# Row sums of the attention weights: part of them moved from ScalarE to GpSimd and VectorE, with pinned orders

## The chip, the cores and the metric

One NeuronCore of a Trainium2 chip runs the whole kernel. TensorE multiplies matrices, VectorE and GpSimd work element by element, ScalarE evaluates functions, SyncE (SP) issues most DMAs. Each engine takes its instructions in order from a queue of its own; semaphores tie the queues together. The metric is the time of one execution in device microseconds; the shown number is the median of several runs.

## The reference

The network has four layers on four images of 128 channels and 64 x 64 pixels: a state-space layer with convolutions, a 3 x 3 convolution, an attention block with expert feed-forward, and a linear attention with expert feed-forward. The change lies in the attention of the third layer alone. An image has 4096 tokens, 16 heads and a width of 8 per head. Query, key and value are the same tensor:

```python
qkv = _qz_ring(heads + rx_theta)
q = jnp.transpose(qkv, (0, 2, 1, 3))
scores = jnp.einsum('bhsd,bhtd->bhst', q, q) / np.sqrt(D)
attn = jax.nn.softmax(scores, axis=-1)
ctx = jnp.einsum('bhst,bhtd->bhsd', attn, q)
```

Since query and key are the same, the matrix of scores is symmetric. Its exponentials are needed once for each pair of tokens, used for both the row and the column, and the softmax needs their sums over both directions.

## The kernel before

`attention` (line 909) runs once per image, between stages (`prepare`, `feed_forward`) that compute the heads and what follows. The 4096 tokens are cut into four blocks of queries, j = 0 to 3, of 1024 tokens, and sixteen blocks of keys, m, of 256 tokens. Only blocks with m >= 4j are computed. A block with m // 4 > j lies off the diagonal ("behind" in the code) and serves both directions; the four with m // 4 = j serve one. `pairs(j)` gives the order of the m: behind a few of the first kind comes one of the diagonal. A head has 16 + 12 + 8 + 4 = 40 steps, of which 24 are "behind"; an image has 16 heads and 640 steps.

One step (loop at line 1073) consists of:

- four matmuls `score` for the 2 x 1024 scores of a pair of key halves, into two PSUM tiles of three;
- two exponentials on ScalarE (line 1094), `ex`, 128 x 1024 each. In "behind" steps each also accumulates the sum of its row into `dacc` (`accum_out`); the chip then runs a second, short instruction that reads the accumulator out;
- in "behind" steps two 32 x 32-block transposes on VectorE (line 1098) into `turned`. A `turned` tile takes the eight transposes of four blocks m, and there are two such tiles;
- `turns` (line 1015): once all eight transposes of a group are made and a step has passed, TensorE multiplies them with values that GpSimd has spread (`turned_v`), one to three `turn`s of four matmuls in a step, eight turns for a group, summed in `acc_ps`. Behind a group's last turn VectorE copies or adds `acc_ps` to `acc` (lines 1006, 1008);
- `weigh` (line 1026) of the step before: the exponentials times values, summed in `ctx_ps` over all m of a j. At the last m of a j the turned sums are added by `place` matmuls, VectorE copies `ctx_ps` to `ctx` (line 1057), and SP stores it with eight DMAs.

`load` (line 921) fetches keys and queries of the next head by 32 DMAs into `raw`, and GpSimd casts them to the matmul type (line 940). `load_values` (line 944) fetches values by four DMAs and spreads them on GpSimd (line 954), three times a head. At the end of an image one reduce over `dacc` (line 1110) gives the sums.

TensorE's order in this stage is the order of the program (`manual_schedule`, line 1207). The orders of the other engines come from the framework's scheduler, which sorts by its own estimates. On VectorE that has put, at the first step of a new j, the two transposes of this step in front of the copy of the `ctx_ps` that was just finished.

Of the kernel before, what the change touches and what calls it, by code (L numbers as in the profile page):

```python
# [9 lines left out]
F32 = mybir.dt.float32  # L10
F32R = mybir.dt.float32r
I32 = mybir.dt.int32
AF = mybir.ActivationFunctionType
ALU = mybir.AluOpType
AX = mybir.AxisListType
PSUM = bass.MemoryType.PSUM

P = 128
NB = 4
HW = 64  # L20
L = HW * HW
CH = 512
# [752 lines left out]
def layer2_attention(K, xd, dpool, w):  # L775

    nc, tc, mm = K.nc, K.tc, K.mm
# [4 lines left out]
    with ExitStack() as ctx:  # L782
# [126 lines left out]
        def attention(qt, dsum, big, work, pssc, psctx, psacc):  # L909
# [11 lines left out]
            def load(h, queues=(nc.sync, nc.sync)):  # L921

                out = []
                for keys in (True, False):
                    t = work.tile([P, L // 2], F32R, name="keys" if keys else "queries")
                    raw = work.tile([P, L // 2], F32, name="raw")
                    n = P if keys else CH
                    for p in range(2):  # L930
                        for c in range(2):
                            for k in range(4):
                                r = unit(p, c).start + HD * k
                                src = head_d[k // 2 if keys else k % 2, HD * h : HD * h + HD]
                                at = p if keys else c
                                queues[not keys].dma_start(
                                    out=raw[r : r + HD].rearrange("d (m s) -> d m s", s=n),
                                    in_=src.rearrange("d (m z s) -> d m z s", z=2, s=n)[:, :, at],
                                )
                    nc.gpsimd.tensor_copy(t, raw)  # L940
                    out.append(t)
                return out

            def load_values(h, j):


                v = work.tile([P, 4 * BT, HD], F32, name="v")
                for a in range(4):
                    nc.sync.dma_start(
                        out=v[32 * a : 32 * a + 32],  # L950
                        in_=value_d[h, :, j].rearrange("s q t d -> s (q t) d"),
                    )
                t = work.tile([P, 4 * BT, 4, HD], F32, name="turned_v")
                nc.gpsimd.tensor_tensor(  # L954
                    t,
                    v.unsqueeze(2).to_broadcast([P, 4 * BT, 4, HD]),
                    quarter.unsqueeze(1).to_broadcast([P, 4 * BT, 4, HD]),
                    ALU.mult,
                )
                return t  # L960
# [8 lines left out]

            steps = [(h, j, m) for h in range(NH) for j in range(NJ) for m in pairs(j)]  # L970
            heads = {0: load(0, (nc.sync, nc.scalar))}
            values = {(0, 0): load_values(0, 0)}
            order = [(h, j) for h in range(NH) for j in range(NJ - 1)]
            cps = psctx.tile([P, CH], F32, name="ctx_ps")
            aps = psacc.tile([P, 2, BT, 32], F32, name="acc_ps")
# [4 lines left out]
            def turn():  # L980

                r, h, j, i, td, _, sums = groups[0]
                if r == 0:
                    sums = groups[0][-1] = aps[:, halves[0] % 2]
                    halves[0] += 1
                groups[0][0] += 1
                tv = values[h, j]
                for g in range(4):
                    n = 4 * r + g
                    q, t = divmod(n, BT)  # L990
                    at = 32 * (4 * t + q)
                    mm(
                        sums[32 * g : 32 * g + 32],
                        tv[:, n].rearrange("p a d -> p (a d)"),
                        td[:, :, at : at + 32],
                        start=r == 0,
                        stop=r == BT - 1,
                    )
                if r < BT - 1:
                    return False  # L1000
                groups.pop(0)
                if i == 1:
                    accs[h] = work.tile([P, NJ - 1, BT, 32], F32, name="acc")
                at = accs[h][:, i - 1]
                if j == 0:
                    nc.vector.tensor_copy(at, sums)  # L1006
                else:
                    nc.vector.tensor_tensor(at, at, sums, ALU.add)
                if i == NJ - 1:
                    after = order.index((h, j)) + 2  # L1010
                    if after < len(order):
                        values[order[after]] = load_values(*order[after])
                return True

            def turns(n, ready):
# [10 lines left out]
            def weigh(h, j, m, exs):  # L1026

                last = m == 4 * j + 3
                first = m == (4 * j + 4 if j < NJ - 1 else 4 * j)
                for p in range(2):  # L1030
                    at = (h * NTT + 2 * m + p) * (HD + 1)
                    for c in range(2):
                        mm(
                            cps[unit(p, c), :],
                            qt[:, at : at + 32],
                            exs[p][:, c, :],
                            start=first,
                            stop=last and j == 0,
                        )
                if not last:  # L1040
                    return
                if j > 0:
                    while any(g[1] == h and g[3] == j for g in groups):
                        turn()
                    for k in range(2):
                        for p in range(2):
                            for c in range(2):
                                a = 2 * p + k
                                mm(
                                    cps[unit(p, c), :].rearrange("r (t a s) -> r t a s", a=4, s=32)[:, :, a],  # L1050
                                    place[:, a, :],
                                    accs[h][:, j - 1, 4 * c : 4 * c + 4],
                                    start=False,
                                    stop=k == 1,
                                )
                u = work.tile([P, CH], F32, name="ctx")
                nc.vector.tensor_copy(u, cps)  # L1057
                for p in range(2):
                    for c in range(2):
                        cols = slice((2 * j + c) * CH, (2 * j + c + 1) * CH)  # L1060
                        r = unit(p, c).start
                        nc.sync.dma_start(out=num_d[p, HD * h : HD * h + HD, cols], in_=u[r : r + HD])
                        nc.sync.dma_start(out=den_d[p, h : h + 1, cols], in_=u[r + HD : r + HD + 1])

            values[order[1]] = load_values(*order[1])


            starts = [n for n, (h, j, m) in enumerate(steps) if m // 4 > j and m % 4 == 0]
# [1 line left out]
            begun = {}  # L1070
            turned = None
            past = None
            for n, (h, j, m) in enumerate(steps):
                keys, queries = heads[h]
                if n == 0 or h != steps[n - 1][0]:
                    if h + 1 < NH:
                        heads[h + 1] = load(h + 1)
                behind = m // 4 > j
                if n in ends:
                    turned = work.tile([P, BT, 2 * CH], F32, name="turned")  # L1080
# [2 lines left out]
                for p in range(2):  # L1083
                    for c in range(2):
# [2 lines left out]
                            keys[unit(p, c), m * P : (m + 1) * P],  # L1087
                            queries[unit(p, c), j * CH : (j + 1) * CH],
                        )
                exs = []  # L1090
                for p in range(2):
                    ex = work.tile([P, 2, CH], F32, name="ex", bufs=6)
                    t = 2 * m + p
                    nc.scalar.activation(  # L1094
                        ex, sps[p], AF.Exp, scale=scale, accum_out=dacc[:, j, h, t : t + 1] if behind else None
                    )
                    if behind:
                        nc.vector.transpose(turned[:, t % BT, :], ex.rearrange("p c s -> p (c s)"))  # L1098
                    exs.append(ex)
                turns(n, lambda g: begun[id(g[4])] < n - 1)  # L1100
                if past is not None:
                    weigh(*past)
                past = (h, j, m, exs)
                if behind and m % 4 == 3:
                    begun[id(turned)] = n
# [1 line left out]
            while groups:  # L1107
                turn()
            weigh(*past)
            nc.vector.tensor_reduce(dsum, dacc.rearrange("p j h t -> p t h j"), AX.X, ALU.add)  # L1110

        def feed_forward(b, dsum, work, psum):
# [75 lines left out]
        for b in range(NB + 1):  # L1188
            with tc.tile_pool(name="l2_big", bufs=1) as big:
# [12 lines left out]
                with (  # L1202
                    tc.tile_pool(name="l2_work", bufs=2) as work,
                    tc.tile_pool(name="l2_pssc", bufs=3, space=PSUM) as pssc,
                    tc.tile_pool(name="l2_psctx", bufs=1, space=PSUM) as psctx,
                    tc.tile_pool(name="l2_psacc", bufs=1, space=PSUM) as psacc,
                    tc.manual_schedule(engines={mybir.EngineType.PE}),
                ):
                    attention(qt, past, big, work, pssc, psctx, psacc)

# [432 lines left out]
```

## Time and profile before

| | |
|---|---|
| median of 3 runs | 11391.87 us (11381.06 to 11405.95) |
| the profiled execution | 11405.55 us, span 11403.8 us |
| the four attention stages | 1424, 1427, 1427, 1425 us |
| busy over the whole span | TensorE 81%, VectorE 64%, ScalarE 66%, GpSimd 23% |
| busy in the second attention stage | TensorE 94%, VectorE 68%, ScalarE 89%, GpSimd 12% |
| granted TensorE clock in it | 0.99 |

PE is TensorE (PEld its weight loads), DVE VectorE, ACT ScalarE, POOL GpSimd, SP SyncE. A row of the largest groups names line, engine, operation, output<-input, shapes and count; then the busy time in us and the mean of one in ns; then how long the engine stood idle ahead of such instructions, and for whom it waited. L89 is the helper for all matmuls, so matmuls are told apart by their tiles. In the view of waits the numbers are us in total, times, and the longest. In the timeline they are the start, the duration, engine, line, operation, tiles, and in brackets the idle time ahead of it.

### The profile page before, as it was taken

The numbers are of one execution on the slowest core, as the hardware profiler recorded it, in microseconds if no ns is written. First come the engines' busy times: TensorE is split into PE (matmuls) and PEld (weight loads), VectorE is DVE, ScalarE is ACT, GpSimd is POOL, SyncE is SP. The second block draws the span as 40 slices with busy tenths as digits, with TensorE's granted clock in tenths as the row PEclk, the third lists the DMA queues.
The fourth block names the chain that finished last, engine by engine and source line by source line (L and its number), as shares of the span: only waits on it lengthen the run. The fifth ranks groups of instructions, "written<-read, shape, count | busy, mean of one in ns | idle before, by whom it ended". The sixth has DMA issues, their size and how long they took to land. (4 is left out here: it accounts for less than half of the span.)

```text
span 11403.8 us, 182690 instructions
## 1 busy us (share of the span) xinstructions
PE 9270.3 (81%) x71376; PEld 3448.3 (30%) x71376; DVE 7274.7 (64%) x7758; ACT 7509.0 (66%) x11610; POOL 2630.9 (23%) x1711
## 2 busy tenths in 40 slices
PE   5777777777759999958999967999967999976766
PEld 2222223222123333323333322333322333323433
DVE  2687687687736666656666655666655666654464
ACT  2564554554428888848888847888846888852331
POOL 0466455565611111121111121111121111110000
PEclk8888878888679999979999979999979999988898
DMA  3322322322122121122211122122122112112103
GB/s 84 89 63 56 95 61 66 86 63 66 49 57 34 32 32 32 34 66 35 37 31 32 24 74 38 32 33 36 24 71 41 31 31 33 31 55 87 49 16 133
DMA packets 524322, 581.50 MB, mean 51 GB/s; under 512 B 106232, under 2 KB 329536, under 8 KB 520896
## 3 DMA queue, kind: packets, MB, share of 16 engines
q1 hardware_dynamic: 520896, 565.61, 21.6%
q8 instruction: 561, 9.19, 0.3%
q10 hardware_dynamic: 2560, 4.20, 0.3%
q14 instruction: 305, 2.50, 0.1%
HBM read 373.96 MB, written 76.55 MB: 40 GB/s over the span
## 5 line engine op out<-in xcount | busy, mean ns | idle before, releaser
L1094 ACT ACTIVATE ex<-score 128x1024 f32<-128x1024 f32 x5120 | 5015.9, 1040 | 665.4 <-PE score L89 657.3
L1098 DVE STREAM_TRANSPOSE turned<-ex 128x1024 f32<-128x1024 f32 x3072 | 3596.9, 1219 | 1595.6 <-ACT ex L1094 1453.1
L89 PE MATMUL ctx_ps<-ex,qt 128*32 128x512 f32 x20480 | 2872.8, 603 | 230.4 <-DVE ctx L1057 229.7
L89 PE MATMUL acc_ps<-turned,turned_v 128*32 128x256 f32 x24576 | 1750.8, 387 | 99.2 <-DVE acc L1006 49.7
L89 PE MATMUL score<-queries,keys 32*128 32x512 f32 x10240 | 1365.0, 500 | 185.4 <-POOL queries L940 182.1
L641 DVE TENSOR_TENSOR_SCAN hs<-decay,carry,hs 128x512 f32<-128x512 f32 x1024 | 1248.0, 1263 | 151.2 <-ACT decay L640 141.9
L640 ACT ACTIVATE decay<-dt,a_neg 128x512 f32<-128x512 f32 x1024 | 699.9, 690 | 883.0 <-DVE hs L641 879.4
L954 POOL TENSOR_TENSOR turned_v<-v,quarter 128x1024 f32<-128x1024 f32 x192 | 456.4, 2378 | 3549.9 <-PE acc_ps L89 3432.7
L89 PEld LDWEIGHTS score<-queries,keys 32*128 32x128 f32 x10240 | 529.3, 183 | 2262.3 <-issue 1589.0
L647 POOL TENSOR_TENSOR hs<-hs,c_sb 128x1024 f32<-128x1024 f32 x512 | 1201.4, 2367 | 49.1 <-DMA c_sb<-c_d 29.4
L89 PEld LDWEIGHTS ctx_ps<-ex,qt 128*32 128x32 f32 x20480 | 683.1, 110 | 832.8 <-DVE ctx L1057 310.3
L89 PEld LDWEIGHTS acc_ps<-turned,turned_v 128*32 128x32 f32 x24576 | 607.3, 108 | 780.2 <-issue 514.9
L89 PE MATMUL y_ps<-hs,pair 128*64 128x512 f32 x2048 | 658.8, 761 | 224.4 <-POOL hs L647 224.3
L637 DVE TENSOR_TENSOR hs<-dtx,b_ps 128x2048 f32<-128x2048 f32 x256 | 581.5, 2271 | 316.8 <-PE b_ps L89 227.8
L1094 ACT ACTIVATION_READ_ACCUMULATOR ex<-score 128x1 f32 x3072 | 680.4, 221 | 0.0
L89 PE MATMUL ln_var<-ln_sq,mean 128*128 128x512 f32 x448 | 296.3, 748 | 220.5 <-ACT ln_sq L104 185.1
L89 PE MATMUL b_ps<-dbc,spread 32*128 32x512 f32 x512 | 343.8, 756 | 149.6 <-DVE hs L637 149.6
L89 PE MATMUL conv<-under,deep 96*32 96x512 f32 x1536 | 283.2, 715 | 74.4 <-DMA under<-xp 54.6
L89 PEld LDWEIGHTS y_ps<-hs,pair 128*64 128x64 f32 x2048 | 138.3, 161 | 674.2 <-POOL hs L647 418.0
L940 POOL CAST keys<-raw 128x2048 fp32r<-128x2048 f32 x64 | 121.1, 1892 | 917.9 <-DMA raw<-head_d 865.2
L644 POOL COPY carry<-hs 128x4 f32<-128x4 f32 x256 | 64.9, 253 | 1108.9 <-DVE hs L641 1096.0
L1057 DVE COPY ctx<-ctx_ps 128x512 f32<-128x512 f32 x256 | 169.7, 663 | 198.5 <-PE ctx_ps L89 198.5
(340 smaller groups left out, 8583.1 us busy)
## 6 DMA issues: line engine op xcount, KB each, us to landing
raw<-head_d SPq DMA_DIRECT2D x1984, 64.0 KB
c_sb<-c_d SPq DMA_DIRECT2D x512, 128.0 KB
dt<-dt SPq DMA_DIRECT2D x128, 256.0 KB
dtx<-dtx SPq DMA_DIRECT2D x128, 256.0 KB
w<-in_L_ffn_weight SPq DMA_DIRECT2D x32, 1024.0 KB
w<-in_L_ffn_weight SPq DMA_DIRECT2D x128, 256.0 KB
under<-xp SPq DMA_DIRECT2D x384, 66.0 KB
under<-fp SPq DMA_DIRECT2D x384, 66.0 KB
```

The costliest lines, as they stand in the source:

```text
L89: self.nc.tensor.matmul(out, lhsT, rhs, start=start, stop=stop)
L637: nc.vector.tensor_tensor(hs, dtx2, bb.unsqueeze(1).to_broadcast([P, NQ, CH]), ALU.mult)
L640: nc.scalar.activation(ex, dt2[:, q, :], AF.Exp, scale=a_neg[:, q, g : g + 1])
L641: nc.vector.tensor_tensor_scan(hs[:, q, :], ex, hs[:, q, :], carry[:, g, q : q + 1], ALU.mult, ALU.add)
L644: nc.gpsimd.tensor_copy(carry[:, g, :].unsqueeze(2), hs[:, :, CH - 1 : CH])
L647: nc.gpsimd.tensor_tensor(at, at, cs.unsqueeze(1).to_broadcast([P, 2, CH]), ALU.mult)
L940: nc.gpsimd.tensor_copy(t, raw)
L954: nc.gpsimd.tensor_tensor(t, v.unsqueeze(2).to_broadcast([P, 4 * BT, 4, HD]), quarter.unsqueeze(1).to_broadcast([P, 4 * BT, 4, HD]), ALU.mult,
L1057: nc.vector.tensor_copy(u, cps)
L1094: nc.scalar.activation(ex, sps[p], AF.Exp, scale=scale, accum_out=dacc[:, j, h, t : t + 1] if behind else None)
L1098: nc.vector.transpose(turned[:, t % BT, :], ex.rearrange("p c s -> p (c s)"))
```

## The change

- 15 of the 24 "behind" steps of a head (`folded`: eight in j=0, four in j=1, three in j=2) no longer accumulate on ScalarE. `fold` has GpSimd add the two halves of each row of the exponentials, 2 x 1024 to 2 x 512, and again to 2 x 256 (`quarters`). Five steps later VectorE reduces these to two columns of `dacc`.
- The two exponentials of a step share one tile, `ex`, of four buffers; before there were six of half the size.
- VectorE and GpSimd now also run in the order of the program in this stage.
- `turns` and `weigh` stand ahead of the exponentials and transposes in the program. TensorE's order stays; on VectorE the copies of `acc_ps` and `ctx_ps` come ahead of that step's transposes.
- Keys and queries are loaded directly into their tiles and cast in place, at steps 28 and 32 of the head ahead (`rounded`); before, they went through `raw`. Values are spread three steps after their loads are issued (`waiting`), where before the scheduler placed it.

```diff
@@ load, load_values
-                    raw = work.tile([P, L // 2], F32, name="raw")
+                    raw = t.bitcast(F32)
...
-                    nc.gpsimd.tensor_copy(t, raw)
                     out.append(t)
                 return out
+
+            def rounded(t):
+
+                nc.gpsimd.tensor_copy(t, t.bitcast(F32))
...
+                return v
+
+            def spread_values(v):
                 t = work.tile([P, 4 * BT, 4, HD], F32, name="turned_v")
@@ turn
-                        values[order[after]] = load_values(*order[after])
+                        waiting.append((now[0] + 3, order[after], load_values(*order[after])))
@@ before the loop
+            folds = []
+
+            def folded(j, m):
+
+                return ((m - 4) % 3 < 2, m % 2 == 0, m % 4 < 3)[j]
+
+            def fold(n, exs, at):
+                hs = work.tile([P, 2, CH], F32, name="folded", bufs=1)
+                qs = work.tile([P, 2, CH // 2], F32, name="quarters", bufs=6)
+                nc.gpsimd.tensor_tensor(hs, exs[:, :, 0], exs[:, :, 1], ALU.add)
+                nc.gpsimd.tensor_tensor(qs, hs[:, :, 0 : CH // 2], hs[:, :, CH // 2 :], ALU.add)
+                folds.append((n + 5, qs, at))
@@ the loop over steps
-                if n == 0 or h != steps[n - 1][0]:
-                    if h + 1 < NH:
+                if h + 1 < NH:
+                    if n % per == 0:
                         heads[h + 1] = load(h + 1)
+                    if n % per in (per - 12, per - 8):
+                        rounded(heads[h + 1][n % per == per - 8])
+                while waiting and n >= waiting[0][0]:
+                    _, at, v = waiting.pop(0)
+                    values[at] = spread_values(v)
...
-                exs = []
+                turns(n, lambda g: begun[id(g[4])] < n - 1)
+                if past is not None:
+                    weigh(*past)
+                exs = work.tile([P, 2, 2, CH], F32, name="ex", bufs=4)
+                aside = behind and folded(j, m)
                 for p in range(2):
-                    ex = work.tile([P, 2, CH], F32, name="ex", bufs=6)
+                    ex = exs[:, p]
                     t = 2 * m + p
+                    summed = behind and not aside
                     nc.scalar.activation(
-                        ex, sps[p], AF.Exp, scale=scale, accum_out=dacc[:, j, h, t : t + 1] if behind else None
+                        ex, sps[p], AF.Exp, scale=scale, accum_out=dacc[:, j, h, t : t + 1] if summed else None
                     )
                     if behind:
                         nc.vector.transpose(turned[:, t % BT, :], ex.rearrange("p c s -> p (c s)"))
-                    exs.append(ex)
-                turns(n, lambda g: begun[id(g[4])] < n - 1)
-                if past is not None:
-                    weigh(*past)
+                if aside:
+                    fold(n, exs, dacc[:, j, h, 2 * m : 2 * m + 2])
+                while folds and folds[0][0] <= n:
+                    _, qs, at = folds.pop(0)
+                    nc.vector.tensor_reduce(at, qs, AX.X, ALU.add)
@@ the stage's pools
-                    tc.manual_schedule(engines={mybir.EngineType.PE}),
+                    tc.manual_schedule(
+                        engines={mybir.EngineType.PE, mybir.EngineType.DVE, mybir.EngineType.Pool}
+                    ),
```

More of the change, by code (lines that the diff above doesn't have):

```diff
@@ L971, in attention @@
             heads = {0: load(0, (nc.sync, nc.scalar))}
-            values = {(0, 0): load_values(0, 0)}
+            for t in heads[0]:
+                rounded(t)
+            values = {(0, 0): spread_values(load_values(0, 0))}
+            waiting = []
             order = [(h, j) for h in range(NH) for j in range(NJ - 1)]
@@ L1035, in weigh @@
                             qt[:, at : at + 32],
-                            exs[p][:, c, :],
+                            exs[:, p, c, :],
                             start=first,
@@ L1063, in weigh @@
                         nc.sync.dma_start(out=den_d[p, h : h + 1, cols], in_=u[r + HD : r + HD + 1])
-            values[order[1]] = load_values(*order[1])
+            values[order[1]] = spread_values(load_values(*order[1]))
+            folds = []
[7 more added lines that the diff above has]
+                folds.append((n + 5, qs, at))
             starts = [n for n, (h, j, m) in enumerate(steps) if m // 4 > j and m % 4 == 0]
@@ L1072, in attention @@
             past = None
+            now = [0]
+            per = len(steps) // NH
             for n, (h, j, m) in enumerate(steps):
+                now[0] = n
                 keys, queries = heads[h]
-                if n == 0 or h != steps[n - 1][0]:
-                    if h + 1 < NH:
+                if h + 1 < NH:
+                    if n % per == 0:
                         heads[h + 1] = load(h + 1)
+                    if n % per in (per - 12, per - 8):
[3 more added lines that the diff above has]
+                    values[at] = spread_values(v)
                 behind = m // 4 > j
@@ L1109, in attention @@
             weigh(*past)
+            for _, qs, at in folds:
+                nc.vector.tensor_reduce(at, qs, AX.X, ALU.add)
             nc.vector.tensor_reduce(dsum, dacc.rearrange("p j h t -> p t h j"), AX.X, ALU.add)
```

## The prediction

> **What bounds the kernel now.** I first read the slices and the largest groups of the profile page. The changed code is the attention stage, which runs four times, once per image. Asked for those four stretches, the trace gives 1424, 1427, 1427 and 1425 us, half of the span. The rest of the kernel isn't touched and I leave it at 11403.8 - 5703 = 5701 us.
>
> ```profile
> core 0: us, PE busy (x) PEld busy (x) DVE busy (x) ACT busy (x) POOL busy (x), PEclk, DMA share, GB/s
> 5148.00:6575.00 1427.00, 1343.70 (x14568) 480.52 (x14562) 967.97 (x928) 1269.86 (x2048) 170.17 (x78) 0.99 0.18 31
> ```
>
> Busy shares in it: TensorE 94%, ScalarE 89%, VectorE 68%, GpSimd 12%. Two engines are near full, so I looked at the groups.
>
> ```profile
> L1094 ACT ACTIVATE ex<-score 128x1024 f32<-128x1024 f32 x5120 | 5015.9, 1040 | 665.4 <-PE score L89 657.3
> L1098 DVE STREAM_TRANSPOSE turned<-ex 128x1024 f32<-128x1024 f32 x3072 | 3596.9, 1219 | 1595.6 <-ACT ex L1094 1453.1
> L89 PE MATMUL ctx_ps<-ex,qt 128*32 128x512 f32 x20480 | 2872.8, 603 | 230.4 <-DVE ctx L1057 229.7
> L89 PE MATMUL acc_ps<-turned,turned_v 128*32 128x256 f32 x24576 | 1750.8, 387 | 99.2 <-DVE acc L1006 49.7
> ...
> L647 POOL TENSOR_TENSOR hs<-hs,c_sb 128x1024 f32<-128x1024 f32 x512 | 1201.4, 2367 | 49.1 <-DMA c_sb<-c_d 29.4
> ...
> L1094 ACT ACTIVATION_READ_ACCUMULATOR ex<-score 128x1 f32 x3072 | 680.4, 221 | 0.0
> ```
>
> ScalarE waits 657.3 us for scores, TensorE 229.7 us for a copy on VectorE. The view of waits says how often:
>
> ```profile
> ACT ex L1094 <- PE score L89: 657.3, 983, 11.1
> ...
> PE ctx_ps L89 <- DVE ctx L1057: 229.7, 188, 2.1
> ```
>
> That is 1.22 us a time, three times a head (64 heads, 192 places). The timeline at one such place, the move from j=1 to j=2:
>
> ```profile
> 5566.33 2.37 DVE L1098 STREAM_TRANSPOSE turned<-ex 128x1024 f32<-128x1024 f32 x2 [0.92 <-ACT ex L1094]
> ...
> 5566.78 0.62 PE L89 MATMUL ctx_ps<-acc,place 128*32 128x128 f32 x16
> ...
> 5567.88 1.94 ACT L1094 ACTIVATE ex<-score 128x1024 f32<-128x1024 f32 x2 [0.58 <-PE score L89]
> 5568.62 0.65 DVE L1057 COPY ctx<-ctx_ps 128x512 f32<-128x512 f32 x1
> ...
> 5569.33 1.07 PE L89 MATMUL ctx_ps<-ex,qt 128*32 128x512 f32 x8 [0.93 <-DVE ctx L1057]
> ```
>
> The sums are ready at 5567.40; their copy stands behind two transposes until 5568.62, and TensorE stands still to 5569.33.
>
> Per step I took the distance between the first exponentials of neighbouring steps, from their starts in the trace, averaged over heads (steps counted 0 to 39). A head lasts 89.25 us. Steps with a transpose and one turn or none last 1.99 us (4, 5, 19, 20, 25, 26, 32, 34), diagonal ones 1.82: ScalarE's pace. Steps with two turns last 2.30 to 2.35: TensorE's pace. The move to a new j costs most: 3.77 (step 1), 3.30 (17), 3.05 (29); step 22 has 2.84. From the timeline TensorE needs 0.43 for scores, 0.95 for context, 0.445 a turn and 0.6 for the place products: 1.38, 1.83, 2.28 with no, one, two turns; 40 x 1.38 + 48 x 0.445 + 3 x 0.6 = 78.4 us a head at least.
>
> **What the Trainium skill says.** "ScalarE: Activation LUTs", What ACT_TABLE_LOAD costs: back-to-back ACTIVATEs overlap by about 93 ns. The trace agrees: 1.04 us each, 0.91 apart without accumulation, 1.00 with it. So a read of the accumulator, 221 ns in its row, costs only 0.09 us of ScalarE's pace. "GPSIMD Engine Reference", 1. Specifications: the SBUF interfaces are shared with VectorE, with contention for VectorE instructions in a 2-port mode or with two SBUF inputs. Transposes have one input, and 145 of them that lie wholly under GpSimd work took 1.21 us, against 1.22 for those clear of it. "VectorE: DVE Perf Modes", Rules for kernel authors: expect 1x of `tensor_reduce`. The trace has one of 512 elements:
>
> ```profile
> L413 DVE TENSOR_REDUCE sm<-sc x32: 651/659/686, 118.9 to 2226.2; 128x32 f32<-128x512 f32 x32
> ```
>
> **The change part by part**, in us a head, times 64.
>
> *Reads removed.* 15 of 24 steps lose two reads: 30 x 0.09 = 2.7 if ScalarE set the pace everywhere. It doesn't where a folded step has two turns (8, 9, 12, 13, 16, 22) or lies in a move (28). Left are 0, 1, 4, 5, 19, 25, 30 and 32: 8 x 0.18 = 1.4. Gain 1.4, between 0.5 and 2.7.
>
> *Copies ahead of transposes.* At steps 0, 16 and 28 the copy is now ahead of the two transposes. It starts when the sums are ready and takes 0.66; meanwhile TensorE has 0.43 of scores and mostly a turn, so about 0.15 of each 1.22 is left. Gain 3 x 1.07 = 3.2; bounds 2 and 3.6. What is late next: transposes of that step, which now wait for TensorE's sums.
>
> *Row sums on VectorE.* 15 reduces at about 0.62 (0.66 less the overlap of neighbours) are 9.3: VectorE goes from 968 to 968 + 240 x 0.62 = 1117 of about 1390 us per image, 80%. Idle time of 1.46 us between transposes covers them in j=2. In j=0, steps 0 to 15 hold 24 transposes 1.17 apart, six reduces and 1.4 of copies, 33.2 us, against 35.4 that these steps last now: no cover to spare. Behind a reduce wait the next transposes and the copy of the accumulators; for both TensorE waits at the first turn of the next group. Three places:
> - Step 16. Six transposes from step 12 on are 7.0, the copy of step 15 0.4, ending some 0.3 after TensorE wants them today. The reduces of steps 13 and 14 stand in front of that copy: 1.2 later.
> - Step 22. Today VectorE is late by 2.84 - 2.28 = 0.56. Now the transposes of step 16 wait for the copy that waits for two turns, and the reduces of 17 and 18 add 1.24; the diagonal step takes up part. Loss 0.7.
> - Step 6. The head's first transposes wait behind the copy, and ScalarE brings step 4 and 5 sooner. Loss 0.6.
>
> Together 2.5; bounds 0.5 (idle time takes most) and 5.5 (a reduce of this form near 1 us, as the `dsum` reduce with its 2.92 us for 1536 elements would give, and every one of them on the path).
>
> *Folds on GpSimd.* 2.37 (the L647 row) + 1.27 (a 128x512 sum on GpSimd, L1182) = 3.64; fifteen are 54.6. With three spreads at 2.38 and two casts at 1.89 that is 65.5 of 87 us. Cost nothing while the exponential four steps later still finds its buffer free. Tightest: step 5 needs the first half of step 1's fold; fold 0, the spread now placed at step 1 and that half are 8.4 after step 0, the exponential is due at 7.5. The 0.9 is hidden, since step 6 waits for transposes anyway. Without that cover: 0.9 a head, 58 us. Bounds 0 and 1.
>
> *Casts and loads.* The loads write keys and queries directly, casts come at steps 28 and 32, in front of those steps' folds. A head's 32 loads take 32 x 0.65 = 21 us of SP's queue, begun when the head before last has finished its scores; they have landed some 35 us before the cast. The queries' cast ends near step 33, needed seven steps later. On SP three value loads now stand in a row ahead of the context stores of j=2; the third waits for a spread at step 38, the stores are ready at 37, and their buffer is next wanted a head later. Nothing; if the loads were late, GpSimd would stop with all folds behind it.
>
> *Batch start.* Each image's first scores wait 45 us for loads and casts (182.1 us in all); these are the same transfers. Nothing.
>
> Sum: 1.4 + 3.2 - 2.5 = 2.1 a head, x 64 = 134 us. The profiled execution took 11405.55 (span 11403.8): 11271. It stood 13.7 above the median of the runs: **11257 us**.
>
> **Rivals.**
> 1. *VectorE has room.* Reduces fall into its idle time and the copies stay prompt. For it: 68% busy now, 1453 us waiting for ScalarE. Against: j=0 has no such room. 1.4 + 3.2 = 4.6, 294 us: 11098.
> 2. *VectorE, in its fixed order, sets the pace* (other side). Place: first turns at steps 6, 16, 22. It decides once the lateness there passes 4.6 a head instead of 2.5. For it: j=0 at 33.2 of 35.4, copies that wait for TensorE with transposes behind them. Against: the measured 0.66. At 5.5 it loses 0.9 x 64 = 58: 11450.
> 3. *GpSimd sets the pace*: needs (87 - 10.9) / 15 = 5.1 a fold where rows say 3.64. At 5.6, 10.9 + 84 = 94.9 a head, 5.7 over today's: 11392 + 365 = 11757.
> 4. *No change*: gain and lateness cancel, 11392.
>
> **How the numbers follow.** Forecast (gains of 30 to 230) 0.53; rival 1 (beyond) 0.24; rival 4 0.07; rival 2 0.13; rival 3 0.03. Within 0.2% (23 us, about what this measurement can tell from no change) 0.07, faster 0.77, slower 0.16. Range: down to 11080, which holds most of rival 1, up to 11430, part of rival 2; about 0.1 is left out on each side. The forecast's own range is 11165 to 11360.
>
> **What would show it.** Right: 1152 reads left; waits of context for its copy from 229.7 to below 60; reduces near 0.66; waits of `acc_ps` for VectorE above 99; steps 4 and 5 at 1.85, steps 1, 17 and 29 together some 3 us shorter, 16 and 22 longer. Wrong: ScalarE waiting for GpSimd at all; transposes above 1.25; step 16 no longer than today (rival 1).

## The result and the profile after

The changed kernel took 11269.95 us in the median of four runs (11248.79 to 11277.42), against 11396.6 in four runs of the kernel before. The ratio is 0.9887, with a 95% interval of 0.9869 to 0.9905: 1.1% faster, 127 us. The forecast was 11257. The profiled execution was the fastest of the four, with a span of 11247.0; the one profiled before was among the slower of its kernel, so the two spans differ by more, 157 us.

The stretches of the four attention stages are now 1391, 1392, 1391 and 1391 us. Their sum of 5565 is 138 under that of before; the other 19 us of the two spans lie outside the attention stages. The second stretch, with the same columns as before:

```profile
core 0: us, PE busy (x) PEld busy (x) DVE busy (x) ACT busy (x) POOL busy (x), PEclk, DMA share, GB/s
5108.00:6500.00 1392.00, 1327.58 (x14569) 482.03 (x14570) 1098.28 (x1167) 1232.73 (x1568) 1046.23 (x558) 1.00 0.19 32
```

VectorE went from 68% to 79% busy, GpSimd from 12% to 75%, and ScalarE stayed at 89% of a shorter stretch. The largest groups of the page after:

```profile
L1129 ACT ACTIVATE ex<-score 128x1024 f32<-128x1024 f32 x5120 | 4917.9, 1027 | 674.6 <-issue 282.4
L1133 DVE STREAM_TRANSPOSE turned<-ex 128x1024 f32<-128x1024 f32 x3072 | 3586.1, 1217 | 504.4 <-ACT ex L1129 375.5
...
L89 PE MATMUL ctx_ps<-ex,qt 128*32 128x512 f32 x20480 | 2817.8, 596 | 22.1 <-DVE ctx L1066 21.4
L89 PE MATMUL acc_ps<-turned,turned_v 128*32 128x256 f32 x24576 | 1750.7, 387 | 215.8 <-DVE acc L1015 161.9
...
L1138 DVE TENSOR_REDUCE dacc<-quarters 128x2 f32<-128x512 f32 x960 | 622.2, 653 | 0.0
```

The context matmuls wait 21.4 us for their copy instead of 229.7, and ahead of the `acc_ps` matmuls TensorE is idle for 215.8, nearly all of it for VectorE, instead of 99.2. Transposes kept their 1.22 us although GpSimd now works beside most of them. The reduces take 0.653.

The distance in us between the first exponentials of neighbouring steps, as in the prediction, shows where it went. It is averaged over the heads of each image but the first and the last. The steps that the text needs are shown, of both kernels and of six of the runs told of below; a head is the sum of all 40 steps.

| step | before | after | order alone | old order | spread behind | reduces at diagonals | held to 21 | sums left out |
|---|---|---|---|---|---|---|---|---|
| 1 | 3.77 | 1.87 | 2.02 | 3.66 | 1.86 | 1.86 | 1.86 | 1.86 |
| 4 | 1.99 | 2.67 | 1.99 | 1.81 | 1.81 | 2.67 | 1.81 | 1.81 |
| 5 | 1.99 | 1.82 | 1.99 | 1.81 | 1.81 | 1.83 | 1.81 | 1.81 |
| 6 | 2.09 | 2.08 | 2.12 | 2.43 | 2.48 | 2.08 | 2.48 | 2.49 |
| 11 | 1.99 | 2.04 | 1.99 | 2.59 | 2.04 | 2.04 | 2.04 | 1.99 |
| 16 | 2.47 | 3.62 | 2.47 | 3.62 | 3.62 | 2.52 | 2.51 | 2.46 |
| 17 | 3.30 | 2.25 | 2.35 | 2.25 | 2.25 | 2.24 | 2.25 | 2.36 |
| 22 | 2.84 | 3.53 | 2.84 | 3.50 | 3.52 | 3.53 | 2.91 | 2.88 |
| 28 | 2.75 | 2.83 | 2.74 | 3.41 | 2.82 | 2.82 | 2.82 | 2.79 |
| 29 | 3.05 | 1.83 | 1.94 | 2.21 | 1.83 | 1.83 | 1.83 | 1.94 |
| 36 | 3.48 | 3.48 | 3.48 | 4.07 | 3.48 | 3.48 | 3.48 | 3.42 |
| head | 89.25 | 86.90 | 85.32 | 90.42 | 86.43 | 85.80 | 84.71 | 84.77 |

The three moves to a new j (steps 1, 17, 29) are 4.2 us a head shorter. Steps 4, 16 and 22 are 2.5 longer, and the others together 0.7 shorter. That makes 2.35 a head; over all heads, the first and last ones too, it is 2.18, or 139 us for 64, as the stretches say. Step 16 in the timeline of the kernel after, VectorE's lines first, TensorE's behind them:

```profile
5488.61 0.64 DVE L1138 TENSOR_REDUCE dacc<-quarters 128x2 f32<-128x512 f32 x1
5489.18 2.36 DVE L1133 STREAM_TRANSPOSE turned<-ex 128x1024 f32<-128x1024 f32 x2
5491.46 0.64 DVE L1138 TENSOR_REDUCE dacc<-quarters 128x2 f32<-128x512 f32 x1
5492.02 0.41 DVE L1015 COPY acc<-acc_ps 128x256 f32<-128x256 f32 x1
...
5490.70 0.51 PE L89 MATMUL score<-queries,keys 32*128 32x512 f32 x4
5492.49 1.07 PE L89 MATMUL acc_ps<-turned,turned_v 128*32 128x256 f32 x16 [1.29 <-DVE acc L1015]
```

Two reduces stand in front of the copy, one of them directly, and TensorE idles 1.29 us for that copy. At step 22 it idles as long, 1.23 in the mean, for the next such copy. Step 4 is late by another engine. ScalarE's line comes first, then GpSimd's:

```profile
5468.12 2.86 ACT L1129 ACTIVATE ex<-score 128x1024 f32<-128x1024 f32 x3 [0.73 <-POOL folded L1084]
...
5459.66 2.38 POOL L1084 TENSOR_TENSOR folded<-ex 128x1024 f32<-128x1024 f32 x1 [10.02 <-ACT ex L1129]
5462.12 1.28 POOL L1085 TENSOR_TENSOR quarters<-folded 128x512 f32<-128x512 f32 x1
5463.37 2.38 POOL L960 TENSOR_TENSOR turned_v<-v,quarter 128x1024 f32<-128x1024 f32 x1
5465.70 2.39 POOL L1084 TENSOR_TENSOR folded<-ex 128x1024 f32<-128x1024 f32 x1
```

The exponential of step 5 reuses the tile of step 1. It starts when GpSimd's fold has read that tile, and that fold stood behind the fold of step 0 and the spread.

### The profile page after: what moved, and what is told of

It is laid out like the page before. It is cut to its first block, busy times and chain, and to the rows that moved or that the text cites. A ratio compares the mean times of both kernels' runs of the same rounds, so it can differ in the third digit from the quotient of the medians.

```text
span 11247.0 us, 183547 instructions
## 1 busy us (share of the span) xinstructions
PE 9199.9 (82%) x71376; PEld 3451.5 (31%) x71376; DVE 7810.3 (69%) x8718; ACT 7359.6 (65%) x9690; POOL 6136.6 (55%) x3631
## 3 DMA queue, kind: packets, MB, share of 16 engines
q14 instruction: 307, 2.51, 0.1%
## 5 line engine op out<-in xcount | busy, mean ns | idle before, releaser
L1129 ACT ACTIVATE ex<-score 128x1024 f32<-128x1024 f32 x5120 | 4917.9, 1027 | 674.6 <-issue 282.4
L1084 POOL TENSOR_TENSOR folded<-ex 128x1024 f32<-128x1024 f32 x960 | 2293.4, 2389 | 1260.2 <-ACT ex L1129 1226.9
L89 PE MATMUL ctx_ps<-ex,qt 128*32 128x512 f32 x20480 | 2817.8, 596 | 22.1 <-DVE ctx L1066 21.4
L89 PE MATMUL acc_ps<-turned,turned_v 128*32 128x256 f32 x24576 | 1750.7, 387 | 215.8 <-DVE acc L1015 161.9
L1085 POOL TENSOR_TENSOR quarters<-folded 128x512 f32<-128x512 f32 x960 | 1231.4, 1283 | 75.3
L1138 DVE TENSOR_REDUCE dacc<-quarters 128x2 f32<-128x512 f32 x960 | 622.2, 653 | 0.0
```

The lines of the kernel that those rows point to most:

```text
L89: self.nc.tensor.matmul(out, lhsT, rhs, start=start, stop=stop)
L1084: nc.gpsimd.tensor_tensor(hs, exs[:, :, 0], exs[:, :, 1], ALU.add)
L1085: nc.gpsimd.tensor_tensor(qs, hs[:, :, 0 : CH // 2], hs[:, :, CH // 2 :], ALU.add)
L1129: nc.scalar.activation(ex, sps[p], AF.Exp, scale=scale, accum_out=dacc[:, j, h, t : t + 1] if summed else None)
L1138: nc.vector.tensor_reduce(at, qs, AX.X, ALU.add)
```

## The experiments

Theory A: the gain is that of the order of the copies; the row sums on GpSimd and VectorE cost more than the removed reads give. Theory B: the gain is that of the reads. Theory C: both share it.

**The order alone.** Against the kernel before:

```diff
+                turns(n, lambda g: begun[id(g[4])] < n - 1)
+                if past is not None:
+                    weigh(*past)
                 exs = []
...
-                turns(n, lambda g: begun[id(g[4])] < n - 1)
-                if past is not None:
-                    weigh(*past)
                 past = (h, j, m, exs)
...
-                    tc.manual_schedule(engines={mybir.EngineType.PE}),
+                    tc.manual_schedule(engines={mybir.EngineType.PE, mybir.EngineType.DVE}),
```

> The kernel before with one part of the change: turns and weigh ahead of the exponentials, VectorE in program order; all 24 row sums stay on ScalarE. Theory A (the gain of the change comes from the copies standing ahead of the transposes, and its row sums on VectorE and GpSimd only cost): the moves at steps 1, 17 and 29 lose 2.0 + 1.05 + 1.14 a head as in the changed kernel, step 16 stays within 0.3 of today's 2.47: about 3.9 a head, 250 us, near 11145. Theory B (the gain comes from the removed accumulator reads): within 25 us of the kernel before. Theory C (both halves share it): 60 to 150 us faster.

Measured: 11152.79 us, ratio 0.9783 (0.9768 to 0.9797): 246 us under the 11398.66 of the kernel before, twice the gain of the whole change. The rows of its context and `acc_ps` matmuls:

```profile
L89 PE MATMUL ctx_ps<-ex,qt 128*32 128x512 f32 x20480 | 2882.7, 597 | 22.2 <-DVE ctx L1057 21.5 <-ACT ex L1097 0.7
L89 PE MATMUL acc_ps<-turned,turned_v 128*32 128x256 f32 x24576 | 1750.8, 387 | 98.7 <-DVE acc L1006 49.7 <-DVE acc L1008 49.0
```

The waits for the context copy are gone as in the changed kernel, and steps 16 and 22 are as before. Theory A stands, B falls. The copies of the accumulators also moved in this run, but the waits for them stayed at 98.7 us, so it is the context copy that counts. Its waits fell by 208 us; where the other 38 of the 246 come from these rows don't show.

**The sums moved, the old order.** Against the changed kernel:

```diff
-                turns(n, lambda g: begun[id(g[4])] < n - 1)
-                if past is not None:
-                    weigh(*past)
                 exs = work.tile([P, 2, 2, CH], F32, name="ex", bufs=4)
...
                     nc.vector.tensor_reduce(at, qs, AX.X, ALU.add)
+                turns(n, lambda g: begun[id(g[4])] < n - 1)
+                if past is not None:
+                    weigh(*past)
```

> The changed kernel with turns and weigh put back behind the exponentials, transposes and reduces: row sums moved, copies in the old place. Theory A: reads give 0.5 a head, steps 4, 16 and 22 lose 0.7 + 1.15 + 0.7, so slower than the kernel before by 2.0 a head, about 11525. Theory B: keeps most of the gain, near 11290. Theory C: near 11340.

Measured: 11499.06 us, ratio 1.009 (1.0075 to 1.0105): slower than the kernel before, by 100 us. Two rows of it:

```profile
L89 PE MATMUL ctx_ps<-ex,qt 128*32 128x512 f32 x20480 | 2823.2, 604 | 130.7 <-DVE ctx L1066 130.0 <-ACT ex L1126 0.7
L89 PE MATMUL acc_ps<-turned,turned_v 128*32 128x256 f32 x24576 | 1750.8, 387 | 326.0 <-DVE acc L1015 191.2 <-DVE acc L1017 128.8
```

The reads are gone here too, and it doesn't help: in this order reduces stand in front of the accumulators' copies at steps 11, 28 and 36 as well, which the table shows late. Step 11:

```profile
5471.31 0.64 DVE L1135 TENSOR_REDUCE dacc<-quarters 128x2 f32<-128x512 f32 x1
5471.88 0.41 DVE L1015 COPY acc<-acc_ps 128x256 f32<-128x256 f32 x1
...
5472.34 0.85 PE L89 MATMUL acc_ps<-turned,turned_v 128*32 128x256 f32 x12 [0.47 <-DVE acc L1015]
```

Steps 17 and 29 are short in this run without the new order: TensorE has already stood still at steps 16 and 28, 1.30 and 1.11 us in the mean, and then finds the context copy nearly done. So what this run loses against the kernel before is at steps 6, 11, 22 and 36. At step 1 TensorE still waits 1.97 for the context copy, where it waited 2.06 before: to fix VectorE's order, without the new place of the copies, doesn't remove that wait. This rules out C as it was put: the moved sums alone gain nothing.

**The spread behind the fold.** Against the changed kernel:

```diff
-                while waiting and n >= waiting[0][0]:
-                    _, at, v = waiting.pop(0)
-                    values[at] = spread_values(v)
                 behind = m // 4 > j
...
                     nc.vector.tensor_reduce(at, qs, AX.X, ALU.add)
+                while waiting and n >= waiting[0][0]:
+                    _, at, v = waiting.pop(0)
+                    values[at] = spread_values(v)
                 past = (h, j, m, exs)
```

> The changed kernel with the spread of values placed behind the fold of its step in GpSimd's order, so that the fold of step 1 no longer waits for it. If step 4's 2.67 us is GpSimd's lateness alone, it falls to 1.82 and 0.85 a head is gained, 54 us, near 11215. If the late transposes of step 4 stand right behind it, step 6 grows as step 4 shrinks and 0.3 to 0.5 a head is left, 20 to 30 us, near 11245. If GpSimd has nothing to do with it, no change, 11270.

Measured: 11253.99 us, ratio 0.9876 (0.9860 to 0.9893). The median is 16 us under that of the changed kernel, within the spread of single runs; the heads, which vary less, are 86.43 against 86.90. Step 4 falls by 0.86 to 1.81, step 6 grows by 0.40. So GpSimd's lateness was real, and right behind it stood late transposes, for which step 6 waits: about half was to be had.

**Reduces at the diagonals.** Against the changed kernel:

```diff
-                while folds and folds[0][0] <= n:
+                while not behind and folds and folds[0][0] <= n:
```

> The changed kernel with the reduces issued in diagonal steps alone (which have no transposes), so that at step 15 and 21 they stand behind the accumulators' copy. If the reduces ahead of that copy are what made steps 16 and 22 longer, these return to about 2.5 and 2.85: 1.8 a head, 115 us, near 11155. If it is the transposes held up by the context copy, step 22 stays near 3.5 and step 16 alone gives 1.15, 74 us, near 11195. If neither, within 20 us of 11270.

Measured: 11192.34 us, ratio 0.9818 (0.9803 to 0.9832), 85.80 a head. Step 16 returns to 2.52, step 22 doesn't. Its VectorE and then one of its TensorE lines, from step 14 to step 22:

```profile
5469.31 0.38 DVE L1015 COPY acc<-acc_ps 128x256 f32<-128x256 f32 x1
5469.62 1.26 DVE L1138 TENSOR_REDUCE dacc<-quarters 128x2 f32<-128x512 f32 x2
...
5472.35 4.61 DVE L1133 STREAM_TRANSPOSE turned<-ex 128x1024 f32<-128x1024 f32 x4
5476.89 1.24 DVE L1138 TENSOR_REDUCE dacc<-quarters 128x2 f32<-128x512 f32 x2
5478.04 4.61 DVE L1133 STREAM_TRANSPOSE turned<-ex 128x1024 f32<-128x1024 f32 x4
...
5469.74 1.07 PE L89 MATMUL acc_ps<-turned,turned_v 128*32 128x256 f32 x16 [0.19 <-DVE acc L1015]
```

At step 15 the copy now comes first, and TensorE's wait for it is 0.19. But step 18 is a diagonal step too: both its reduces stand where they stood, between the transposes of 17 and 19. So this run shows the cause for step 16 alone. The second number of the expectation fits, but its reason, the context copy, was not tested by it.

**Both edits.** Spread behind the fold and reduces at the diagonals.

> The changed kernel with both edits: spread behind the fold of its step, reduces in diagonal steps alone. If the two losses are independent, 2.35 + 1.1 + 0.47 a head under the kernel before: steps 4, 6 and 16 at 1.81, 2.48 and 2.5, 85.3 a head, near 11160. If one of them only hides the other, no better than 11192.

Measured: 11168.17 us, ratio 0.9804 (0.979 to 0.9819), 85.32 a head: 1.58 under the changed kernel, the sum of 1.10 and 0.47. The two losses are independent.

**No reduce at step 18.** Against the run with both edits:

```diff
-                while not behind and folds and folds[0][0] <= n:
+                while not behind and (j, m) != (1, 4) and folds and folds[0][0] <= n:
```

> As the run with both edits, and no reduce at step 18: the three that are due wait for step 21, behind the accumulators' copy. Theory: step 22 is late because two reduces stand ahead of the transposes of 19 and 20; it returns from 3.53 to about 2.85, 0.7 a head, 44 us, near 11115, under the run with the order alone. Rival: step 22 is late because the context copy holds the transposes of step 16 up; it stays at 3.5, near 11160.

Measured: 11122.64 us, ratio 0.9765 (0.975 to 0.9779), 84.71 a head. Step 22 goes to 2.91.

```profile
5452.50 4.62 DVE L1130 STREAM_TRANSPOSE turned<-ex 128x1024 f32<-128x1024 f32 x4
5457.57 4.62 DVE L1130 STREAM_TRANSPOSE turned<-ex 128x1024 f32<-128x1024 f32 x4 [0.46 <-ACT ex L1126]
5462.12 0.38 DVE L1015 COPY acc<-acc_ps 128x256 f32<-128x256 f32 x1
5462.43 1.85 DVE L1135 TENSOR_REDUCE dacc<-quarters 128x2 f32<-128x512 f32 x3
```

The transposes of step 19 now wait for their exponential; VectorE is no longer behind. The context copy still stands in front of step 16's transposes, as it does in the order alone with its 2.84 at step 22, so it does no harm by itself. The two reduces did.

**The sums left out.** The order alone, without any sum for the 15 steps; this run doesn't compute the whole result. `folded` is the function of the changed kernel. Against the run with the order alone:

```diff
-                        ex, sps[p], AF.Exp, scale=scale, accum_out=dacc[:, j, h, t : t + 1] if behind else None
+                        ex, sps[p], AF.Exp, scale=scale, accum_out=dacc[:, j, h, t : t + 1] if behind and not folded(j, m) else None
```

> The order alone, and the row sums of the same 15 of 24 steps left out of the computation altogether: no accumulation on ScalarE, no fold, no reduce. It shows what removing the accumulator reads is worth at best on top of the order. Theory: 0.9 to 1.1 a head, 60 to 70 us under the order alone, near 11090. If reads were worth their 2.7 a head, 170 us, near 10980. If nothing, 11153.

Measured: 11116.74 us, ratio 0.9759 (0.9744 to 0.9773), 84.77 a head: 0.55 a head or 36 us under the order alone. That is all the reads are worth here, half of what was expected (0.9 to 1.1 a head), though the rows show 1920 x 221 ns = 424 us of them. The table and one row tell why:

```profile
L89 PE MATMUL acc_ps<-turned,turned_v 128*32 128x256 f32 x24576 | 1750.7, 387 | 117.9 <-DVE acc L1006 52.9 <-DVE acc L1008 52.1 <-DVE turned L1105 12.5
```

Steps 4 and 5 win 0.36, and step 6 gives 0.37 back: it has two turns of TensorE's work to do, and this row names waits for `turned`, which that of the order alone doesn't.

**Nothing folded.** The changed kernel with all its other edits, and all sums on ScalarE. Against the changed kernel:

```diff
-                aside = behind and folded(j, m)
+                aside = False
```

> The changed kernel with no step folded: all 24 row sums on ScalarE, but loads in place, casts at steps 28 and 32, spreads three steps later, shared exponential tiles, GpSimd pinned. Theory: these other edits are worth nothing, so the time of the order alone, 11153 within 20 us. Rival: they cost or gain: outside that.

Measured: 11152.78 us, ratio 0.9787 (0.977 to 0.9803), 85.16 a head. It is the time of the order alone: loads in place, later casts, later spreads, shared exponential tiles and GpSimd's fixed order are together worth nothing. The run held to step 21 has four times (11120.87 to 11129.11) that all lie under these four (11140.59 to 11158.44): moved with care, the sums gain 30 us, of the 36 that leaving them out gains. That version is the fastest that computes everything, 273 us under the kernel before.

## Why the prediction was right

The time and the direction came out as forecast, 2.35 us a head against 2.1, and so did the mechanism in the main: the copies' new place gains, and the moved sums take a good part back at the first turns of later groups. That the sum is so close is in part luck. The runs with one part each give 3.93 + 0.55 - 2.13 = 2.35 where the forecast had 3.2 + 1.4 - 2.5: its three errors, 0.7 too little, 0.85 too much and 0.4 too much taken off, nearly cancel.

- *Copies ahead of transposes, 3.2.* Right in mechanism, too small: 3.93 in the run with the order alone. The 1.22 us a time is a mean of unlike waits: 2.06 at step 1, 0.74 at 17, 0.92 at 29. I left 0.15 of each standing; the steps fell by 1.75, 0.95 and 1.11, more than these waits together. In the changed kernel the waits are 21.4 us, where below 60 was forecast.
- *Reads removed, 1.4.* Mis-sized: 0.55. The term counted eight steps at ScalarE's pace, each for itself. But steps 4 and 5 run into step 6, where TensorE has two turns to do and waits for transposes. In j=2, with the sums left out, TensorE's scores follow each other every 1.86 us with no idle time between its instructions, so that its own pace is the next floor.
- *Row sums, -2.5.* Measured 86.90 - 84.77 = 2.13, the distance to the run without these sums. Nearly the same, 2.19, is between the changed kernel and the version in which the reduces and the spread are out of the way. Step 16 was forecast at 1.2 and cost 1.10, by the reduces in front of the copy; step 22 at 0.7 and cost 0.61. That step's reason held in part: the two reduces make it late, the context copy in front of step 16 doesn't.
- *Folds on GpSimd, nothing.* This step failed. The prediction saw the exponential of step 5 late by 0.9 behind fold, spread and fold, and held it hidden under step 6's late transposes, which it charged with 0.6. It was the other way round: the lateness was as forecast, 0.86 (2.67 at step 4 against 1.81 with the spread out of the way), but it was visible, and the late transposes were hidden behind it. It said itself that ScalarE waiting for GpSimd would show it wrong, and 43.2 us of such waits stand in the trace. There are no others of weight. ScalarE's 282.4 us under `issue`, for which no releaser is shown, and 48.7 that the view of waits puts down to GpSimd's cast, are waits for TensorE: nearly all of these exponentials start within 0.1 us of the end of a score matmul, and all at least 0.4 us after GpSimd's last instruction ended. Since one of two delays that overlap was charged, the sum came out nearly right by luck: steps 4 to 6 are 0.5 longer together, and taking the spread away gave 0.47.
- *Casts, loads, batch start, nothing.* Right, by the run with nothing folded.

Rival 1, that VectorE has room, was wrong for this order of reduces, and right for another: held back to the right steps the same 15 reduces fit, and a head is 4.54 shorter than before, where the rival had 4.6. The prediction also read the overlap of neighbouring exponentials from a mean: 1.04 less 0.91 is 0.13. Taken where ScalarE has waited and doesn't accumulate, they last 1.02 and start 0.92 apart, an overlap of 0.10, nearer to the figure it is compared with.

## What to carry to other kernels

In an engine that works in order, what a small instruction costs depends on what stands behind it: fifteen reduces of 0.65 us cost 1.7 us a head where TensorE waited for copies behind four of them, and nothing measurable once those were held back by a few steps. When a change has several parts, run each alone: here one part gave 246 us and the other, as placed, took about half of that back. And price a removed wait by the next floor of the steps around it, not step by step.

## What was not expected of the hardware

Nothing in the durations went against the forecast. With GpSimd 75% busy beside it, VectorE's transposes took 1.217 us in the mean against 1.219 before, and GpSimd's sums of 128 x 1024 took 2.389 against 2.367 of a like row. The work that was moved onto idle time was itself as cheap as its rows said. Its price was in what stood behind it.
